# Slots of a macaron block: where the layer norm runs, and how tokens and attention weights are turned

## The chip, the cores and the metric

The kernel runs on one core of a Trainium2 chip. The metric is the device time of one execution in microseconds (us). The kernel before took 2431.72 us, the median of three runs (2429.35 to 2433.34). One further execution was profiled; its time is 2431.14 us and the profile's span of it is 2429.4 us.

## The reference

The input x is 16 sequences of 512 tokens of width 256, all in float32. The block is a macaron: x gets half of a slot FFN, then causal attention, then half of the same slot FFN again; each of the three works on a layer norm of x without scale and shift.

```python
x = x + 0.5 * ffn(layernorm(x)); x = x + attn(layernorm(x)); x = x + 0.5 * ffn(layernorm(x))

def ffn(h):                                      # h: 512 tokens x 256, 16 slots, 16 heads of 16
    o = slot_query + mha(slot_query, h, h)       # slots attend to tokens ("dispatch")
    o = o + experts(layernorm(o))                # one gated expert of width 1024 per slot
    return mha(h, o, o)                          # tokens attend to the slots ("combine")
```

What the change touches is the dispatch: for every sequence, 256 rows of scores (16 heads times 16 slots) against 512 tokens, a softmax over the tokens, and the weighted sum of the normalized tokens.

## The kernel before, in words

`ffn(n, ...)` runs twice, as n = 0 ahead of the attention and as n = 1 behind it. Each has three stages: the slots (`slots_and_experts`, its first `with` block), the experts (`experts`), and the combine (`combine`). The change is in the slots stage; a few of its lines reach the others.

**Slots stage.** A loop over i takes one sequence b at each step, in a software pipeline three steps deep. A sequence x[b] lies in SBUF with tokens on the 128 partitions (4 groups of 128 tokens, 256 wide). For one sequence the stage does this:

- `token_stats` (L194, L195): VectorE's mean and variance of each group of 128 tokens, four pairs of instructions. For n = 1 the attention has done them already. `pair_rstd` turns the variances of two sequences into 1/std: a square root by ScalarE (L199) and a reciprocal by VectorE (L200).
- `normalized` (L218): h = (x - mean) * rstd, four VectorE instructions of 128x256.
- `width_first` (L226 to L230): the normalized sequence is turned so that its width lies on the partitions: eight transposes of 128x128 by TensorE into two PSUM banks `p_hT`, copied to `hT` by ScalarE (first half, L228) and by VectorE (second half, L230).
- `slot_weights`: for each half c of the 256 score rows, TensorE's scores `p_ds` (L436), VectorE's row maximum (L438), two small GpSimd instructions (L439, L440), ScalarE's exponential with row sums (L441); then VectorE's reciprocal (L443) and GpSimd's scaling of both halves (L445). The result `at` has score rows on the partitions.
- `weights_transposed` (L454 to L460): `at` is turned so that tokens lie on the partitions: eight transposes of 128x128 by TensorE, four to a PSUM bank, copied to `atT` by ScalarE (L458) and VectorE (L460).
- `slot_sums` (L467): TensorE's weighted sums `p_z`, from `h` and `atT`; VectorE copies them to `zT` (L469).

Every fourth sequence `gathered` (L481) multiplies four sequences' sums by the value weights into `moT`. `hT` is kept for the combine: `queries(b)` (L359) makes the tokens' queries from it.

**Order.** TensorE's order is the order of the program text. The other engines and the DMA queue of SyncE (SP) are ordered by a planner in the slots stage. Nearly all DMAs are issued on SP, which takes them one after another. A DMA holds one of eight completion semaphores in turn, so an issue also waits until the DMA eight places ahead of it has landed.

**Weights of the experts.** Each expert has three matrices of 1 MB; eleven buffers hold them. `EARLY` of the buffers exist from the stage's start and are filled there by `load.more(EARLY)`; the other `BUFS - EARLY` lie in memory that the slots stage uses, and are filled when it has ended. The expert loop takes `queries` as fillers, one to an expert (`2 <= e < 11`, and from `e >= NS` on).

**The attention**, between the two, already turns its weights in another way: VectorE transposes 32x32 blocks (L866), and `move` (L889) places them by 16 DMAs from SBUF to SBUF, each from 32 partitions to 32 partitions, 160 KB. Its `enter` (L746) normalizes with ScalarE, with `scale = rstd` and `bias = -mean * rstd`.

Of the kernel before, what the change touches and what calls it, by code (L numbers as in the profile page):

```python
# [9 lines left out]
F32 = mybir.dt.float32  # L10
AF = mybir.ActivationFunctionType
ALU = mybir.AluOpType
# [18 lines left out]
EW = NC * F  # L31
EARLY, BUFS = 7, 11

# [14 lines left out]
def macaron_kernel(ctx: ExitStack, tc: tile.TileContext, a: dict, out: bass.AP):  # L48
# [19 lines left out]
    def by_width(t):  # L68
        return t.rearrange("p (c s) -> p c s", c=NC)

    xin = a["attn_x"].rearrange("b (t p) d -> b p t d", p=P)
# [26 lines left out]
    with tc.tile_pool(name="setup", bufs=1) as su:  # L98
# [44 lines left out]
        for c in range(NC):  # L143
# [6 lines left out]
                            pattern=[[-1, S]], channel_multiplier=1)  # L150
    def more_constants(su):

# [12 lines left out]
        for k, nm in enumerate(("e_b1", "e_bg")):  # L165
            br = su.tile([NS * NQ, QW], F32, tag=f"br{k}", name=f"br{k}", bufs=1)
            nc.sync.dma_start(br, a[nm].rearrange("e (q i) -> (e q) i", q=NQ))
            brs.append(br)
# [17 lines left out]

    mvs, rstds = {}, {}

# [13 lines left out]
    def pair_stats(g):  # L202
        for b in range(g * PB, (g + 1) * PB):
            for t in range(NT):
                token_stats(b, t)

    def pair_rstd(g, parts=1):
        rstds[g] = small.tile([P, PB * NT], F32, tag=f"rstd{g}", name=f"rstd{g}", bufs=1)
        n = PB * NT // parts
        for i in range(parts):  # L210
            inverse_std(rstds[g][:, i * n:(i + 1) * n], mvs[g][:, i * n:(i + 1) * n, 1], n, f"g{g}_{i}")

    def normalized(pool, b, bufs):

        h = pool.tile([P, NT, D], F32, tag="h", name=f"h{b}", bufs=bufs)
        for t in range(NT):
            i = (b % PB) * NT + t
            nc.vector.tensor_scalar(h[:, t, :], xs[b][:, t, :], mvs[b // PB][:, i, 0:1],  # L218
                                    rstds[b // PB][:, i:i + 1], ALU.subtract, ALU.mult)
        return h  # L220

    def width_first(h, b, hT, c):

        pt = ps(f"p_hT{b}_{c}")
        for t in range(NT):
            nc.tensor.transpose(pt[:, t * P:(t + 1) * P], h[:, t, c * P:(c + 1) * P], ident)  # L226
        if c == 0:
            nc.scalar.copy(hT[:, c, :], pt)  # L228
        else:
            nc.vector.tensor_copy(hT[:, c, :], pt)  # L230

# [71 lines left out]
    def slots_and_experts(n, ss, load, w, wvm, rows, hTs, kT, vT):  # L303
# [49 lines left out]
        def queries(b):  # L353

            pqs = []
            for c in range(NC):
                pq = ps(f"p_cq{b}_{c}")
                for k in range(NC):
                    nc.tensor.matmul(pq, w["c_Wq"][:, k, c * P:(c + 1) * P], hTs[b][:, k, :],  # L359
                                     start=(k == 0), stop=(k == NC - 1))  # L360
                pqs.append(pq)
            qT = by_width(place(b, f"cq{n}_"))
            for c in range(NC):
                bias = bcol[:, R_CBQ + c:R_CBQ + c + 1]
                if c == 0:
                    nc.scalar.activation(qT[:, c, :], pqs[c], AF.Identity, bias=bias)
                else:
                    nc.vector.tensor_scalar(qT[:, c, :], pqs[c], bias, 1.0, ALU.add, ALU.mult)
            hTs[b] = qT

        with tc.tile_pool(name=f"disp{n}", bufs=2) as dp:
            hs, ats, zT = {}, {}, None
            constants = more_constants(dp) if n == 0 else None
            tail = None
            load.more(EARLY)

            def norm(b):

                if b >= NB:
                    return  # L380
                if b % PB == 0 and (n == 0 or b >= 2 * PB):
                    pair_rstd(b // PB, PB if b == 0 else 1)
                hs[b] = normalized(dp, b, 4)
                if n == 0 and b % PB == 0 and b + PB < NB:
                    pair_stats(b // PB + 1)

            if n == 0:
                pair_stats(0)
            norm(0)
            norm(1)  # L390
            for i in range(NB + 2):
                if i < NB:
                    hTs[i] = by_width(place(i, f"hT{n}_"))
                    for c in range(NC):
                        width_first(hs[i], i, hTs[i], c)
                if i > 2:
                    atT = weights_transposed(dp, i - 2, ats.pop(i - 2))
                if 0 <= i - 1 < NB:
                    ats[i - 1] = slot_weights(dp, i - 1, hTs[i - 1])
                if i == 2:  # L400
                    atT = weights_transposed(dp, 0, ats.pop(0))
                if i == 5 and n == 0:
                    constants()
                if i > 0:
                    norm(i + 1)
                if i >= 2:
                    b = i - 2
                    if b % GB == 0:
                        if b > 0:
                            gathered(b // GB - 1, zT, moT, wvm)  # L410
                        zT = dp.tile([P, NC, FH, GB, NS], F32, tag="zT", name=f"zT{b}", bufs=1)
                    slot_sums(b, zT, hs.pop(b), atT)
                    if b == NB // 2:
                        tail = half_of_slots(0)
                    if b == NB // 2 + 1:
                        tail()
            queries(0)
            gathered(NB // GB - 1, zT, moT, wvm)
            queries(1)
            tail = half_of_slots(1)  # L420
        with tc.tile_pool(name=f"late{n}", bufs=1) as lw, tc.tile_pool(name=f"exp{n}", bufs=2) as ep:
            load.late = lw
            load.more(BUFS - EARLY)
            queries(2)
            queries(3)
            tail()
            experts(ep, load, w, hET, oT, kT, vT, [lambda b=b: queries(b) for b in range(4, NB)])

    def slot_weights(dp, b, hT):
        at = dp.tile([P, NC, S], F32, tag="at", name=f"at{b}")  # L430
        rsum = small.tile([P, NC], F32, tag="rsum", name=f"rsum{b}")
        mx = small.tile([P, NC], F32, tag="nmx", name=f"nmx{b}")
        for c in range(NC):
            psc = ps(f"p_ds{b}_{c}")
            for k in range(NC):
                nc.tensor.matmul(psc, qk[:, k, c * P:(c + 1) * P], hT[:, k, :], start=(k == 0), stop=(k == NC - 1))  # L436

            nc.vector.tensor_reduce(mx[:, c:c + 1], psc, AX.X, ALU.max)  # L438
            nc.gpsimd.tensor_tensor(mx[:, c:c + 1], mx[:, c:c + 1], sbias[:, c:c + 1], ALU.add)  # L439
            nc.gpsimd.tensor_tensor(mx[:, c:c + 1], sbias[:, c:c + 1], mx[:, c:c + 1], ALU.subtract)  # L440
            nc.scalar.activation(at[:, c, :], psc, AF.Exp, bias=mx[:, c:c + 1], accum_out=rsum[:, c:c + 1])  # L441
        rinv = small.tile([P, NC], F32, tag="rinv", name=f"rinv{b}")
        nc.vector.reciprocal(rinv, rsum)  # L443
        for c in range(NC):
            nc.gpsimd.tensor_scalar(at[:, c, :], at[:, c, :], rinv[:, c:c + 1], 1.0, ALU.mult, ALU.mult)  # L445
        return at

    def weights_transposed(dp, b, at):
        atT = dp.tile([P, NT, FH * NS], F32, tag="atT", name=f"atT{b}", bufs=1)
        for t0 in range(0, NT, 2):  # L450
            pt = ps(f"p_atT{b}_{t0}")
            for t in range(2):
                for c in range(NC):
                    nc.tensor.transpose(pt[:, t * 256 + c * P:t * 256 + (c + 1) * P],  # L454
                                        at[:, c, (t0 + t) * P:(t0 + t + 1) * P], ident)
            dst = atT[:, t0:t0 + 2, :].rearrange("p t q -> p (t q)")
            if t0 == 0:
                nc.scalar.copy(dst, pt)  # L458
            else:
                nc.vector.tensor_copy(dst, pt)  # L460
        return atT

    def slot_sums(b, zT, h, atT):
        pz = ps(f"p_z{b}")
        for c in range(NC):
            for t in range(NT):
                nc.tensor.matmul(pz[:, c * 256:(c + 1) * 256], h[:, t, c * P:(c + 1) * P], atT[:, t, :],  # L467
                                 start=(t == 0), stop=(t == NT - 1))
        nc.vector.tensor_copy(zT[:, :, :, b % GB, :], pz.rearrange("p (c h q) -> p c h q", c=NC, h=FH))  # L469

# [18 lines left out]
    def experts(ep, load, w, hET, oT, kT, vT, fillers):  # L489
# [77 lines left out]
        for e in range(NS + 3):  # L567
# [7 lines left out]
            if 0 <= e - 3 < NS:  # L575
                onto_slots(e - 3)
            if (2 <= e < 11 or e >= NS) and fillers:
                fillers.pop(0)()
# [139 lines left out]
    def attention(qp, wq, wk, wv, wo, cos, sin, row):  # L718
# [4 lines left out]
        nu = len(units)  # L723
        hTs, hs, qs, ks, vs, oTs, prTs, shifts, stds = {}, {}, {}, {}, {}, {}, {}, {}, {}

# [7 lines left out]
        def scales(g, std):  # L733

            n = PB * NT
            rstds[g] = small.tile([P, n], F32, tag=f"rstd{g}", name=f"rstd{g}", bufs=1)
            shifts[g] = small.tile([P, n], F32, tag="shift", name=f"shift{g}", bufs=2)
            nc.vector.reciprocal(rstds[g], std)
            nc.vector.scalar_tensor_tensor(shifts[g], mvs[g][:, :, 0], -1.0, rstds[g], ALU.mult, ALU.mult)

# [317 lines left out]
```

## Time and profile before

| what | value |
|---|---|
| median of three runs | 2431.72 us |
| time of the profiled execution | 2431.14 us |
| its span | 2429.4 us |
| slots stage, n = 0: last `p_z` ends | 174.5 us |
| slots stage, n = 1: first `p_hT` starts, last `p_z` ends | 2014.0 us, 2166.2 us |
| DMA moved | 323.18 MB, mean 133 GB/s |
| mean granted TensorE clock | 0.983 |

The page of the profile has the busy time of each engine, the span in 40 slices, the DMA queues, the chain of work that ended last, and the costliest groups of instructions. A group line reads: source line, engine, operation, out<-in, partitions x elements, number, then busy time and mean of one instruction, then the idle time ahead of it and what ended it. A float32 matmul of the program stands as two instructions in the trace: "x8" for `p_ds` is four matmuls (a transpose stands as one).

### The profile page before, as it was taken

To read this page: it belongs to the slowest core of one execution; us is meant where nothing else is said; L and a number is where in the kernel's file an instruction comes from. 1 tells how busy PE (TensorE), PEld (TensorE's weight loads), DVE (VectorE), ACT (ScalarE), POOL (GpSimd) and SP (SyncE) were. 2 spreads that over 40 slices of the span, in tenths; PEclk is the share of its full clock that TensorE was granted. 3 is DMA by queue.
4 is the path that set the end of the run, shared out by engine and by line. 5 is a ranking of instruction groups with operands and counts; after the bars stand their busy time and mean duration, and the time that the engine had idled before them with its cause. 6 is when DMAs were issued, how large, how long until landed. Compare 5 with 4: busy or idle time off the path is not lost.

```text
span 2429.4 us, 42489 instructions
## 1 busy us (share of the span) xinstructions
PE 2349.0 (97%) x14720; PEld 1475.6 (61%) x14720; DVE 1777.7 (73%) x4687; ACT 1069.4 (44%) x2919; POOL 1065.3 (44%) x1692
## 2 busy tenths in 40 slices
PE   7999889899999999999999999999999979999899
PEld 5765479555555655555656555555555546765488
DVE  8542278778888888888888888888888855542287
ACT  4332233345555555554545545545555433322233
POOL 2220044555564655555656555655556432210053
PEclk9999999999999999999999999999999989999899
DMA  8009852246464555455554545454646454019734
GB/s 308 1 9 370 332 142 78 44 88 138 93 134 102 125 114 117 110 121 112 115 123 104 129 107 120 107 125 102 134 94 138 102 125 167 1 72 397 276 109 135
DMA packets 142477, 323.18 MB, mean 133 GB/s; under 512 B 37236, under 2 KB 84408, under 8 KB 134072
## 3 DMA queue, kind: packets, MB, share of 16 engines
q1 hardware_dynamic: 141676, 319.93, 49.5%
q8 instruction: 117, 1.92, 0.3%
q14 instruction: 96, 0.79, 0.1%
q10 hardware_dynamic: 588, 0.54, 0.1%
HBM read 135.84 MB, written 16.78 MB: 63 GB/s over the span
## 4 chain that ended last, share of the span: by engine, by line
PE 83%; DVE 3%; DMA 2%; SPq 2%; ACT 1%; issue 1%; POOL 0%; DVEq 0%; POOLq 0%; ACTq 0%
PE p_as L831 12%; PE p_av L900 11%; PE p_k L771 9%; PE p_v L792 9%; PE p_q L771 8%; PE p_ay L916 8%; PE p_cq L359 5%; PE p_cy L648 4%; PE p_u L509 2%; PE p_cs L617 2%; PE p_z L467 2%; PE p_ds L436 2%; SPq L889 2%; PE p_y L536 1%; DVE sq L866 1%; PE p_catT L638 1%
## 5 line engine op out<-in xcount | busy, mean ns | idle before, releaser
L851 POOL TENSOR_SCALAR pr<-pr,ars 128x512 f32<-128x512 f32 (+3 forms) x1024 | 523.5, 532 | 655.0 <-DVE ars L848 655.0
L843 ACT ACTIVATE pr<-pr,amn 128x512 f32<-128x512 f32 (+3 forms) x1024 | 561.6, 550 | 462.6 <-DVE amn L839 462.5
L839 DVE CUSTOM_DVE_ANT_0 pr<-p_as,causal 128x512 f32<-128x512 f32 (+3 forms) x1024 | 434.3, 485 | 97.8 <-PE p_as L831 96.5
L866 DVE STREAM_TRANSPOSE sq<-pr 128x768 f32<-128x768 f32 (+2 forms) x448 | 381.6, 906 | 17.4 <-issue 12.8
L831 PE MATMUL p_as<-k,q 32*128 32x512 f32 (+3 forms) x4096 | 332.5, 449 | 3.6 <-POOL k L782 3.6
L900 PE MATMUL p_av<-prT,v 128*64 128x512 f32 (+3 forms) x2048 | 296.7, 443 | 20.4 <-DMA prT<-sq 14.7
L831 PEld LDWEIGHTS p_as<-k,q 32*128 32x128 f32 x4096 | 180.2, 185 | 131.6 <-issue 52.0
L900 PEld LDWEIGHTS p_av<-prT,v 128*64 128x64 f32 x2048 | 141.7, 139 | 181.5 <-issue 158.6
L792 PEld LDWEIGHTS p_v<-wv,ahT 128*128 128x128 f32 x1024 | 189.2, 190 | 98.7 <-issue 45.8
L792 PE MATMUL p_v<-wv,ahT 128*128 128x256 f32 x1024 | 248.5, 386 | 0.0
L916 PE MATMUL p_ay<-wo,aoT 128*128 128x256 f32 x1024 | 238.3, 386 | 0.1
L771 PE MATMUL p_k<-ahT,wk 128*128 128x512 f32 x512 | 236.9, 605 | 0.0
L771 PE MATMUL p_q<-ahT,wq 128*128 128x512 f32 x512 | 230.5, 592 | 0.2 <-ACT ahT L757 0.2
L916 PEld LDWEIGHTS p_ay<-wo,aoT 128*128 128x128 f32 x1024 | 189.3, 190 | 31.3 <-ACT aoT L907 0.6
L843 ACT ACTIVATION_READ_ACCUMULATOR pr<-pr,amn 128x1 f32 x1024 | 191.5, 187 | 0.0
L907 ACT ACTIVATE aoT<-p_av,bcol 128x512 f32<-128x512 f32 x128 | 88.0, 687 | 197.9 <-PE p_av L900 197.8
L771 PEld LDWEIGHTS p_k<-ahT,wk 128*128 128x128 f32 x512 | 92.1, 189 | 126.2 <-issue 114.2
L595 POOL TENSOR_TENSOR kbd<-kT,own 128x256 f32<-128x256 f32 x32 | 19.7, 618 | 309.7 <-DVE kT L562 273.5
L771 PEld LDWEIGHTS p_q<-ahT,wq 128*128 128x128 f32 x512 | 97.1, 190 | 95.8 <-issue 86.3
L648 PE MATMUL p_cy<-vw,catT 128*128 128x256 f32 x512 | 122.5, 383 | 3.0 <-ACT catT L640 3.0
L467 PE MATMUL p_z<-atT,h 128*128 128x256 f32 x512 | 120.2, 389 | 3.6 <-ACT atT L458 3.6
L795 ACT COPY v<-p_v 128x512 f32<-128x512 f32 x128 | 73.4, 573 | 104.9 <-PE p_v L792 104.9
(153 smaller groups left out, 3305.2 us busy)
## 6 DMA issues: line engine op xcount, KB each, us to landing
prT<-sq SPq DMA_DIRECT2D x1024, 160.0 KB
w<-in_e_W_dram SPq DMA_DIRECT2D x64, 1024.0 KB
w<-in_e_Wg_dram SPq DMA_DIRECT2D x32, 1024.0 KB
out_dram<-x SPq DMA_DIRECT2D x64, 256.0 KB
xl<-in_attn_x_dram SPq DMA_DIRECT2D x16, 512.0 KB
xl<-out_dram SPq DMA_DIRECT2D x16, 512.0 KB
x<-in_attn_x_dram SPq DMA_DIRECT2D x15, 512.0 KB
wq<-in_attn_Wq_dram SPq DMA_DIRECT2D x16, 64.0 KB
```

Of the source, the lines that this page charges most:

```text
L359: nc.tensor.matmul(pq, w["c_Wq"][:, k, c * P:(c + 1) * P], hTs[b][:, k, :], start=(k == 0), stop=(k == NC - 1))
L467: nc.tensor.matmul(pz[:, c * 256:(c + 1) * 256], h[:, t, c * P:(c + 1) * P], atT[:, t, :], start=(t == 0), stop=(t == NT - 1))
L648: nc.tensor.matmul(py[:, t * D:(t + 1) * D], atT[:, c, t * P:(t + 1) * P], vws[b][:, c, :], start=(c == 0), stop=(c == NC - 1))
L771: nc.tensor.matmul(pq, self.w[:, k, at:at + P], hTs[self.b][:, k, :], start=(k == 0), stop=(k == NC - 1))
L792: nc.tensor.matmul(pv[:, t * 256:(t + 1) * 256], hTs[b][:, k, (t0 + t) * P:(t0 + t + 1) * P], wv[:, k, hg * HG * DQ:(hg + 1) * HG * DQ], s ...
L831: nc.tensor.matmul(banks[j][:, at:at + w], q[n][j * 32:(j + 1) * 32, i * P:(i + 1) * P], k[n][j * 32:(j + 1) * 32, :w], start=(n == 0), st ...
L839: nc.vector.tensor_tensor_reduce(out=self.at(i, j), in0=banks[j][:, at:at + w], in1=causal[:, S - w:], scale=-1.0 / math.sqrt(DQ), scalar= ...
L843: nc.scalar.activation(self.at(i, j), self.at(i, j), AF.Exp, bias=self.mn[:, i, j:j + 1], scale=-1.0, accum_out=self.rs[:, i, j:j + 1])
L851: nc.gpsimd.tensor_scalar(self.at(i, j), self.at(i, j), self.rs[:, i, j:j + 1], 1.0, ALU.mult, ALU.mult)
L866: nc.vector.transpose(view(self.sq, j * blocks * SQ + dst[0] * SQ, [(blocks * SQ, nh)] + [(s * SQ, n) for s, (_, n) in zip(dst[1:], of)] + ...
L900: nc.tensor.matmul(po[j * DQ:(j + 1) * DQ, :].rearrange("d (a f) -> d a f", a=NSQ)[:, :, t * SQ:], vs[u][:, t, head * DQ:(head + 1) * DQ], ...
L916: nc.tensor.matmul(py[:, t * D:(t + 1) * D], oTs[u][:, pair, (t0 + t) * P:(t0 + t + 1) * P], wo[:, hg * (HG // 2) + pair, :], start=(pair ...
```

## The change

It does five things in the slots stage.

1. The layer norm of all sequences but the first two goes from VectorE to ScalarE (`normalized`), as in the attention; `pair_shift` makes the bias.
2. `at` is no longer turned by TensorE. A new class `Squares` has VectorE transpose 32x32 blocks of a 128x1024 tile into `sq`, writes `sq` to a buffer in device memory by one DMA of 512 KB (`away`, three buffers), and reads it back by four DMAs of 128 KB, each to 32 partitions. Each partition gets four pieces of 1 KB from one read.
3. `h` is turned in the same way into `hT`, for sequences from the fifth on for n = 0 and from the third on for n = 1; the first ones (`direct`) still go through TensorE. `hT`, and what reads it, is laid out by blocks of 32.
4. VectorE, ScalarE, GpSimd and SP follow the program text in the loop (`manual_schedule`). The statistics of sequence i + 4 stand in step i. `zT` is copied by ScalarE.
5. `EARLY` goes from 7 to 6, and the early expert matrices are issued one to a step, in steps 1 to 6, where all seven were issued ahead of the loop. `queries(0)` stands ahead of the last `p_z`, one `queries` more is made before the expert loop, and one filler less is in it.

Step i of the new loop issues on SP, in this order: the four reads of `hT` of i + 1, the write of `at` of i - 1, the write of `h` of i + 2, the four reads of `at` of i - 1, and in steps 1 to 6 one expert matrix. The core of the diff:

```diff
-EARLY, BUFS = 7, 11
+EARLY, BUFS = 6, 11
...
+    class Squares:
+        def __init__(self, pool, away, name, src, outer, inner):
+            n = outer * inner * SQ
+            sq = pool.tile([P, NSQ, n], F32, tag="sq", name=f"sq{name}", bufs=2)
+            nc.vector.transpose(sq.rearrange("p k (i o x) -> p o i k x", i=inner, o=outer),
+                                src.rearrange("p (o i k y) -> p o i k y", o=outer, i=inner, k=NSQ))
+            self.mem = away.tile([P, NSQ, n], F32, tag="away", name=f"away{name}")
+            nc.sync.dma_start(self.mem, sq)
+
+        def onto(self, dst):
+            for k in range(NSQ):
+                nc.sync.dma_start(dst[k * SQ:(k + 1) * SQ].rearrange("y (a f) -> y a f", a=NSQ),
+                                  self.mem.rearrange("(a y) k f -> k y a f", a=NSQ)[k])
...
+            if b < PB:
+                nc.vector.tensor_scalar(h[:, t, :], xs[b][:, t, :], mvs[b // PB][:, i, 0:1], rstd,
+                                        ALU.subtract, ALU.mult)
+            else:
+                nc.scalar.activation(h[:, t, :], xs[b][:, t, :], AF.Identity, bias=shifts[b // PB][:, i:i + 1],
+                                     scale=rstd)
...
-            load.more(EARLY)
...
+            with tc.manual_schedule(engines={mybir.EngineType.DVE, mybir.EngineType.Activation,
+                                             mybir.EngineType.Pool, mybir.EngineType.SP}):
+                for i in range(NB + 2):
+                    if i + 1 in turned:
+                        t = place(i + 1, f"hT{n}_")
+                        hTs[i + 1] = by_squares(t)
+                        turned.pop(i + 1).onto(t)
+                    if i + 1 < direct:
+                        width(i + 1)
+                    if i + 2 < NB:
+                        hs[i + 2] = normalized(dp, i + 2, 5)
+                    if 0 <= i - 1 < NB:
+                        back = Squares(dp, away, f"a{i - 1}", at.rearrange("p c s -> p (c s)"), NC, NT)
+                    stats = [(i + 2 * PB, t) for t in range(NT)] if n == 0 and i + 2 * PB < NB else []
+                    for one in stats[:1]:
+                        token_stats(*one)
+                    def between():
+                        if direct <= i + 2 < NB:
+                            turned[i + 2] = Squares(dp, away, f"h{i + 2}", hs[i + 2].rearrange("p t d -> p (t d)"),
+                                                    NT, NC)
+                    if i < NB:
+                        at, scaled = slot_weights(dp, i, hTs[i], between)
+                    if 0 <= i - 1 < NB:
+                        atT = dp.tile([P, NT * FH * NS], F32, tag="atT", name=f"atT{i - 1}", bufs=2)
+                        back.onto(atT)
...
+                    for one in stats[1:3]:
+                        token_stats(*one)
+                    if i < NB:
+                        scaled()
+                    for one in stats[3:]:
+                        token_stats(*one)
...
+                    if 0 < i <= EARLY:
+                        load.more()
...
+                        if b == NB - 1:
+                            queries(0)
+                        slot_sums(b, zT, hs.pop(b), ats.pop(b))
...
-            if (2 <= e < 11 or e >= NS) and fillers:
+            if (2 <= e < 10 or e >= NS) and fillers:
```

`between` runs after the first half's exponential in `slot_weights`, so VectorE's order in a step is: transpose of `at` of i - 1, one pair of statistics, maximum of the first half, transpose of `h` of i + 2, maximum of the second half, two pairs of statistics, reciprocal, one pair.

## The prediction

> **What bounds the kernel now.** I read the page's engine line first, then the chain of work that ended last in order of time, then the timeline of SP's issues, then the busy time and DMA share by stretches.
>
> ```profile
> PE 2349.0 (97%) x14720; PEld 1475.6 (61%) x14720; DVE 1777.7 (73%) x4687; ACT 1069.4 (44%) x2919; POOL 1065.3 (44%) x1692
> ```
>
> TensorE (PE) is busy nearly all the time, so work taken off it pays at once if nothing else becomes late. The chain in the second slots stage (n = 1):
>
> ```profile
> 2035.24 0.87 PE p_hT L226 x8
> 2036.12 0.87 PE p_atT L454 x8
> 2036.99 3.44 PE p_ds L436 x8
> 2040.42 3.45 PE p_z L467 x16
> 2043.88 0.87 PE p_hT L226 x8
> ...
> 2162.47 3.72 PE p_z L467 x16
> ```
>
> A sequence costs 2043.88 - 2035.24 = 8.64 us, all of it PE, and 1.74 of it are the two turns. The stage ends with the last p_z, at 2166.2; in the first (n = 0) it is 170.78 + 3.72 = 174.5. Behind it:
>
> ```profile
> 170.78 3.72 PE p_z L467 x16
> ...
> 274.23 10.53 DMA w<-in_e_Wg_dram
> ```
>
> So the experts end on their weights, not on PE. The first late weight is issued when the stage's memory is free, 4.6 us after the last p_z, and the DMAs then run full to 284.8: 41 MB in 105.7 us, 2.6 us each. What counts is therefore **when the last p_z ends**, and every MB that is not loaded before. SP's timeline:
>
> ```profile
> 39.01 0.59 SPq L167 DMA_DIRECT2D br<-in_e_bg_dram  x1
> ...
> 179.12 0.33 SPq L291 DMA_DIRECT2D w<-in_e_Wg_dram  x1
> ```
>
> and, from the attention, where 16 DMAs of 160 KB go to 32 partitions each:
>
> ```profile
> 713.03 10.04 SPq L889 DMA_DIRECT2D prT<-sq  x16
> ```
>
> At the start SP is taken up with the input and some twenty small constants until 39.6 us. The columns of the next view end with granted clock, DMA share and GB/s:
>
> ```profile
> 719.00:721.00 2.00, 2.00 (x15) 0.88 (x8) 1.93 (x7) 0.56 (x2) 2.00 (x4) 1.00 1.02 213
> 240.00:260.00 20.00, 20.00 (x180) 9.79 (x178) 5.34 (x15) 5.74 (x11) 0.00 (x0) 1.00 0.99 377
> ```
>
> With the DMAs full, 32-partition moves give 213 GB/s, weights to 128 partitions 377.
>
> **PE.** Removed: 16 turns of at per stage and 12 (n = 0) or 14 (n = 1) of h: 58 x 0.87 = 50.5 us. A step is then 3.44 + 3.45 = 6.9 us. p_av, which already reads blocks of 32, takes 4.46 us for 10240 columns (x32 in the chain), no slower a column than p_ds (3.44 for 4096), so I cost the new layout at nothing.
>
> **VectorE.** A 128x1024 transpose is 1.20 us in the attention (L866). In a step: two of these (2.4), two maxima (0.69 each), and for n = 0 four pairs of statistics (0.41 + 0.17 each); the norm and three copies leave it. More telling is a loop in the given order: transpose of at, maximum, transpose of h, maximum (1.2 + 0.69 + 1.2 + 0.69 = 3.8), then from the second maximum over GpSimd, the exponential, the reciprocal and the scaling back to the next transpose of at. In the tail of before this took 2161.14 - 2158.06 = 3.1 us. Sum 6.9 to 7.0; with the pair of statistics inside the loop 7.6 for n = 0. So VectorE alone allows 7.0 and 7.6, and the saving of PE would mostly stand.
>
> **ScalarE.** Four norms at about 0.52 (three in 1.57 us in the attention, L746), two exponentials with sums (0.88 each), one copy (0.69): 4.6 us; for n = 0 two table loads of 1.28 and a root per two steps make 6.0. Below 7.6, so it is covered; were it not, at most 0.4 a step.
>
> **SP, the step that decides.** Per step SP issues, strictly in order, four reads of hT, the write of at, the write of h, then four reads of at, which wait until the write of at has landed. The next write of at stands behind the next four reads of hT. The loop from one write of at to the next is **landing of the write + eight issues**; the issue of the second write is hidden in the landing, and the transposes are ready earlier (with 7.4 us steps VectorE has at ready some 5 us ahead).
>
> - An issue: 10.04 / 16 = 0.63 us for the 32-partition DMAs; the 512 KB loads xl of the combine take 0.37 + 0.04 of gap = 0.41. The new reads have 32 partitions like the one and come from memory like the other; I take the middle, 0.52. Eight: 4.2 (3.3 to 5.0).
> - Landing, from the completion marks in the trace: a 256 KB write out_dram<-x issued alone at 584.42 had landed after 2.14 us, its bytes in 0.75 us of full DMA. Twice the bytes: 2.9 alone. Right behind four 128 KB reads (the four first ones of x landed 2.1 to 2.8 after issue) it comes to some 3.2. Bounds 2.8 and 4.2.
>
> Without a weight a step is 3.2 + 4.2 = 7.4 us: over PE's 6.9, under the old 8.64. For n = 0 VectorE's 7.6 stands above it.
>
> **A weight in the step.** In steps 1 to 6 a 1 MB weight is issued behind the reads of at, so the reads of hT and the next write queue behind it. That DMAs of this queue wait for each other the trace shows: a 256 KB write issued 0.43 us after a 512 KB load landed after 4.6 us (at 2404.68), not 2.1. The first weight of before landed 5.2 us after its issue. Issued 2.6 us ahead of the write it lands 2.6 after the write's issue; the four reads and the write itself add about 3.0: landing 5.6. Such a step is 5.6 + 4.2 + 0.5 = **10.3 us**, longer than the old 8.64. Before, the seven weights were issued at once and cost PE nothing.
>
> **Sum, first stage.** SP reaches the first write of at not before 39.6. Second write: 39.6 + 2.8 + 2.1 + 0.5 = 45.0. It has a weight right ahead (5.9 to land), and the first reads of hT follow: 45.0 + 5.9 + 2.1 + 0.5 + 2.1 = 55.6. Five loaded steps: 107.1. Eight of 7.6: 167.9. To the end: landing 3.2, four issues 2.1, the last read's landing 1.8, p_z 3.7: 178.7, against 174.5: **+4.2**.
> **Second stage.** The first scores end at 2024.2, and scaling (3.85) and transpose put the first write at 2029.8. Next: + 3.2 + 2.1 + 0.5 + 2.1 = 2037.7. Six loaded steps: 2099.5. Eight of 7.4: 2158.7. End: 2169.5 against 2166.2: **+3.3**.
> **Experts.** One early MB less: 2 x 2.6 = **+5.2**. The moved queries gain nothing, as the experts end on DMAs; were these not the end, a query is 3.44 us.
> Together +12.7 on the profiled 2431.14: **2444 us** (the median is 0.6 above the profiled time).
>
> With issue 0.41 and landing 2.8 the steps are 7.6, 7.0 and 9.5 (loaded), the stages end 2.1 and 6.9 earlier, the sum is -3.8: 2427. With 0.63 and 4.2 (reads at 213 GB/s hold up the write) they are 9.2 and about 12, the stages end 29 and 31 later: 2496.
>
> The row of 213 GB/s above has 32 partitions on both sides; a read from memory to 32 is not in the trace. The Trainium skill, page "SBUF — State Buffer", section "Door 1: The DMA port swizzle", says that partitions 0 to 31 reach only half of the ports, about 218 GB/s. By that, the eight reads of a step (1.05 MB) need 4.8 us, more than their issues, a step would be about 8.0 and my estimate of the sum some 17 us more; by the row of 377 GB/s they need 2.8 and hide.
>
> **Rivals.**
> 1. *The transfers hide* (faster). If a waiting read holds up less than I think, or the weights are spread over idle DMA time, the steps are VectorE's 7.6 and 7.0 throughout. The first stage then saves some 13 us, the second 22, less 5: about 2401. For it: DMA share is 0.01 in this stage before (80 to 160 us), and 2.1 MB per step at 377 GB/s is 5.6 us of 7.0. Against it: SP's order and the two landings in series.
> 2. *It cancels*: shorter plain steps pay for longer loaded steps, within 0.2% (about what a measurement of this kernel can tell from no change): 2431.
> 3. *The reads run at the 32-partition rate*: steps of 8.0 to 9.2, 2460 to 2496.
>
> Decided by one number, the plain step: at 7.0 and with loaded steps of 9.5 the change breaks even; below, it gains.
>
> **Chances.** Forecast (2437 to 2460) 0.48; cancels 0.15; hides 0.25; rate 0.12. Slower by over 0.2%: 0.60; within: 0.15; faster: 0.25. The range, 2405 to 2482, leaves out the far part of rival 1 (0.12) and of rival 3 (0.05).
>
> **What would show it.** Steps of p_ds in the chain: 10 us in steps 2 to 7 and 7.4 to 7.6 later, PE waiting on DMAs of hT and atT (right), or 6.9 to 7.0 with VectorE or PE in the chain (rival 1). SP should wait on the landing of "away" writes for about 3 us a step. The first read of at near 42 us; weights landing 5 us after issue. I am wrong if the reads are issued in 0.4 us, if a 512 KB write lands in 2.5 us behind reads, or if a weight does not hold up what follows.

## The result and the profile after

| | before | after |
|---|---|---|
| median beside each other, us | 2432.53 (2429.35 to 2434.44) | 2469.10 (2466.77 to 2474.31) |
| ratio, 95% interval | | 1.0161 [1.014, 1.0182] |
| time of the profiled execution, its span | 2431.14, 2429.4 | 2474.31, 2472.6 |
| mean granted TensorE clock | 0.983 | 0.974 |
| last `p_z` ends, n = 0 | 174.5 | 195.1 |
| first `p_hT` starts, last `p_z` ends, n = 1 | 2014.0, 2166.2 | 2034.2, 2209.0 |
| DMA moved | 323.18 MB | 384.00 MB |

The kernel became 1.6% slower. All of it lies in the two slots stages: the first ends 20.6 us later, the second is 174.8 us long instead of 152.2 (22.6 more), what lies between them (1839.1 against 1839.5) and behind the last `p_z` (263.6 against 263.2) is unchanged. 20.6 + 22.6 = 43.2, the difference of the two spans. The profiled execution is the slowest of its four; the medians differ by 36.6.

The engine line of the page after, to be held against the one of before:

```profile
PE 2320.4 (94%) x14256; PEld 1431.5 (58%) x14256; DVE 1758.6 (71%) x4557; ACT 1112.7 (45%) x3007; POOL 1064.3 (43%) x1692
```

TensorE's busy time did fall, by 28.6 us, and the kernel is slower all the same: what was taken off TensorE is less than the waits that came. It fell by less than the 50.5 us of turns that went, among other things because matmuls that stayed took longer: the same 256 instructions of `p_ds` were busy for 126.1 us in place of 118.2, the 512 of `p_z` for 124.3 in place of 120.2. The chain of work that ended last, in the second stage, in one step with a weight (start, length, what):

```profile
2058.66 0.02 SPq L259
2058.67 0.03 issue
2058.70 7.74 DMA awaya<-sqa
2066.45 0.02 issue
2066.46 0.32 SPq L263
...
2068.25 0.43 SPq L325
...
2070.56 6.88 DMA hT<-awayh
2077.43 0.14 issue
2077.57 5.38 PE p_ds L505 x8
```

Where before each sequence was 8.64 us of TensorE, the chain is now made of transfers: 7.74 us for the write of turned attention weights, then reads of `atT` (L263), then the weight (L325), then 6.88 us for the last read of `hT`, and only then the scores. The waits of SP in the steps 2 to 7 of that stage (engine, line, what it waited for: us in total, times, longest):

```profile
SPq L263 <- DMA awaya<-sqa: 40.3, 6, 7.6
```

6.7 us a step go into waiting for a write to land. And the busy time by stretches; the first row is these six steps, the second five plain ones behind them (the columns end with granted clock, DMA share and GB/s):

```profile
2058.70:2134.60 75.90, 49.68 (x208) 29.11 (x208) 23.83 (x36) 24.88 (x55) 12.88 (x37) 0.93 0.80 249
2142.40:2184.00 41.60, 37.94 (x193) 24.49 (x192) 22.52 (x40) 21.32 (x45) 10.58 (x30) 1.00 0.84 256
```

The reader is to see two things. A loaded step takes 75.9 / 6 = 12.65 us, a plain one 8.3. And in both the 16 DMA engines are busy for 80 to 84% of the time, though they move only 249 to 256 GB/s; with weights alone it was 377 GB/s at a share of 0.99 (in the kernel before) and 413 at 1.03 (in run e2 below). For the same busy time about a fifth less is moved.

The trace also has every packet (the piece that one DMA engine moves at a time) with its size and length. Summed over the 16 engines and divided by 16, a loaded step holds 4.1 us of reads (1 KB packets, mean 63 ns), 2.7 us of writes (4 KB, 167 ns) and 3.2 us of the weight: 10.0 of the 12.65. A plain one has 4.2 and 2.7: 6.9 of 8.3.

### The profile page after: what moved, and what is told of

Same layout as the page of the kernel before. It is cut to its first block, busy times and chain, and to the rows that moved or that the text cites. A ratio compares the mean times of both kernels' runs of the same rounds, so it can differ in the third digit from the quotient of the medians.

```text
span 2472.6 us, 41964 instructions
## 1 busy us (share of the span) xinstructions
PE 2320.4 (94%) x14256; PEld 1431.5 (58%) x14256; DVE 1758.6 (71%) x4557; ACT 1112.7 (45%) x3007; POOL 1064.3 (43%) x1692
## 2 busy tenths in 40 slices
DMA packets 184238, 384.00 MB, mean 155 GB/s; under 512 B 41876, under 2 KB 118744, under 8 KB 175832
## 4 chain that ended last, share of the span: by engine, by line
PE 80%; DMA 9%; DVE 4%; SPq 4%; ACT 1%; issue 1%; POOL 0%; DVEq 0%; ACTq 0%; POOLq 0%
PE p_as L892 12%; PE p_av L961 11%; PE p_v L853 9%; PE p_k L832 9%; PE p_ay L977 9%; PE p_q L832 9%; DMA awaya<-sqa 5%; PE p_cq L393 4%; PE p_cy L710 4%; PE p_u L571 2%; PE p_cs L679 2%; SPq L263 2%; PE p_z L529 1%; PE p_y L598 1%; PE p_catT L700 1%
## 5 line engine op out<-in xcount | busy, mean ns | idle before, releaser
L927 DVE STREAM_TRANSPOSE sq<-pr 128x768 f32<-128x768 f32 (+2 forms) x448 | 381.6, 906 | 16.7 <-issue 12.7
L529 PE MATMUL p_z<-atT,h 128*128 128x256 f32 x512 | 124.3, 398 | 45.7 <-DMA atT<-awaya 36.1
L505 PE MATMUL p_ds<-hT,qk 128*128 128x512 f32 x256 | 126.1, 640 | 24.7 <-DMA hT<-awayh 24.7
L529 PEld LDWEIGHTS p_z<-atT,h 128*128 128x128 f32 x512 | 99.3, 199 | 78.3 <-issue 46.8
```

The lines of the kernel that those rows point to most:

```text
L505: nc.tensor.matmul(psc.rearrange("p (a n) -> p a n", a=NSQ), qk[:, k, c * P:(c + 1) * P], hT[:, k], start=(k == 0), stop=(k == NC - 1))
L529: nc.tensor.matmul(pz[:, c * 256:(c + 1) * 256].rearrange("p (c g i) -> p c g i", c=NC, g=NSQ), h[:, t, c * P:(c + 1) * P], atT[:, t], sta ...
L927: nc.vector.transpose(view(self.sq, j * blocks * SQ + dst[0] * SQ, [(blocks * SQ, nh)] + [(s * SQ, n) for s, (_, n) in zip(dst[1:], of)] + ...
```

## Theories and experiments

**A.** A step is the landing of the write plus eight issues, in SP's order: the theory of the prediction. **B.** The step is set by the time that all its packets take on the shared DMA engines, in whatever order they are issued. **C.** The order that is now given to VectorE, ScalarE and GpSimd makes the loop late. The kernels below were compared with the kernel before on the same chip; the ratios are to it.

**Run e1, the write ahead of the reads.**

```diff
-                    if i + 1 in turned:          # the four reads of hT
-                        ...
                     if i + 2 < NB:
                         hs[i + 2] = normalized(dp, i + 2, 5)
                     if 0 <= i - 1 < NB:
                         back = Squares(dp, away, f"a{i - 1}", ...)
+                    if i + 1 in turned:
+                        ...
```

> Edit: in each step the write of at is issued ahead of the four reads of hT instead of behind them; nothing else moves. Theory A (the loop on SP decides: landing of the write of at, then eight issues, where 4.3 us and 8 x 0.46 us were measured in plain steps, 7.7 us landing in steps with a weight): four issues leave the loop, a plain step falls from 8.0 to 7.0 to 7.6 (the next limit is VectorE's loop), a step with a weight from 12.3 to about 10.3; the time falls by about 30 us, to 2439. Theory B (the DMA engines are simply full, DMA share 0.8 to 0.9 in these steps, and the order of the issues does not matter): steps stay within 0.5 us of 8.0 and 12.3, the time falls by 8 us at most. Theory C (the given order of the compute engines, with VectorE and ScalarE waiting on TensorE in their order, is what lengthens the steps): no change within 5 us.

Measured: 2460.45 us, ratio 1.0124 [1.0099, 1.0149], some 9 us less than the change, though the two intervals touch. Most plain steps became 6.6 to 8.4 (three were 10.1 to 12.8), but the loaded ones stayed at 9.7 to 13.8, and the landing of the write in them grew to between 7.0 and 11.4 us. The order matters little, as B says.

**Run e2, the weights behind the loop.**

```diff
-                    if 0 < i <= EARLY:
-                        load.more()
+                    if i == NB:
+                        load.more(EARLY)
```

> Edit: the six early expert matrices are issued together in step 16, behind the last reads of at, and not one to a step in steps 1 to 6. Theory A: all steps are plain ones of 8.0 us, six times 4.3 us less per stage (26), the matrices then land partly behind the stage's end and cost some 5 us of it back per stage: about -40 us, 2429. Theory B: the bytes of the weights leave the full steps, 6 x 2.6 us less per stage, and return at the end: -15 to -20 us. Theory C: no change of the steps, and later weights: 5 to 15 us slower.

Measured: **2422.95 us, ratio 0.997 [0.996, 0.998]**: 46 us less than the change, and 0.3% faster than the kernel before. The same six steps of the second stage, by stretches, and SP's waits in them:

```profile
2046.80:2094.50 47.70, 43.51 (x208) 27.81 (x208) 23.82 (x36) 24.38 (x55) 12.70 (x36) 1.00 0.84 264
```

```profile
SPq L263 <- DMA awaya<-sqa: 18.2, 6, 3.6
```

A step is 7.95 us in place of 12.65, and TensorE is busy for 91% of it in place of 65%. In this stage the six weights cost 4.7 us each where they stood: more than the 2.6 of an undisturbed MB, and more than their packets' 3.2. The second stage is now 143.9 us long (152.2 before), the first ends at 178.6 (174.5 before). So turning through memory does gain, in the second stage, 8.3 us; what made the kernel slower is where the weights went.

**Run e3, `h` by TensorE.** `direct = NB`: only `at` goes through memory.

> Edit: h of all sequences is turned by TensorE as before the change; only the attention weights go through VectorE and memory. Theory A: the loop on SP has only four issues and an emptier queue (landing 2.8 + 4 x 0.46 + write, 4.7 us, with a weight about 8.7), so plain steps are TensorE's 7.75 us: about 2420, below the kernel before. Theory B: half the bytes, the same steps as in A. Theory C: VectorE and ScalarE still wait in their given order: steps of 8 us and more, and a time of 2440 or more.

Measured: 2440.92 us, ratio 1.0053 [1.0033, 1.0074]. Half of the loop's bytes and issues are gone and plain steps are 7.8 (TensorE's own 6.9 + 0.87), yet a loaded step is mostly still 8.3 to 11.4 (one is 14.3) with landings of 6 to 9 us, and the forecast of A is missed by 21 us. The time is the one that C gave (2440 or more), but not by C's way, since the plain steps are below 8. DMA share fell to 0.61 (2060 to 2120 us): here the engines are not full, and the step with a weight is long all the same. B alone does not explain that; a write that lands late behind the weight would.

**Run e4, the planner orders the engines.** The `manual_schedule` of the slots loop is taken away.

> Edit: only TensorE's order is given; the planner orders VectorE, ScalarE, GpSimd and SP in the slots stage as before the change. The planner puts SP's four reads of at ahead of the four reads of hT and both writes and the weight ahead of both; the loop on SP keeps its eight issues and the landing. Theory A: the same steps, 2469 within 10 us (a weight now lies ahead of the reads of at, too). Theory B: the same, 2469 within 5 us. Theory C: the steps fall to TensorE's 6.9 to 7.5 us, 2440 or less.

Measured: 2446.49 us (2433.48 to 2453.76), ratio 1.0068 [1.0049, 1.0088], about 23 us less than the change, between the expectations. The planner puts the writes and the weight ahead of the reads; landings of writes fall to 3.8 to 5.5 (one is 6.9), the reads of `at` behind the weight take 5 to 8 us, and loaded steps are 9.4 to 12.2. So the given order is worth a part of the loss, and no order that was tried makes a weight in the step free.

**Run e5, both edits** (e1 and e2).

> The two edits before together: no weight inside the loop (all six are issued behind the last step), and the write of the turned attention weights is issued ahead of the four reads of hT. Theory A (a step is the write's landing plus eight issues, all in SP's order): the write no longer stands behind four issues of 0.47 us nor behind their 0.5 MB, so a plain step falls from about 7.9 to TensorE's 6.9 or VectorE's 7.6, some 0.5 to 0.9 us a step over 26 steps: about 2403 to 2412 us, ratio 0.990 to 0.993 to the kernel before. Theory B (the DMA engines' throughput sets the step: 2.1 MB a step at 260 to 300 GB/s is 7 to 8 us in whatever order): no gain over the version with the weights at the end alone, 2419 to 2426.

Measured: 2423.04 us, ratio 0.9979 [0.9968, 0.999], no better than e2 alone: the number that B gave. But the waits show another reason than B's. SP's waits over the whole second stage, first of this run, then of the changed kernel:

```profile
SPq L259 <- DVE sqa L256: 32.4, 16, 6.4
...
SPq L263 <- DMA awaya<-sqa: 6.2, 5, 2.6
```

```profile
SPq L263 <- DMA awaya<-sqa: 65.2, 16, 7.6
```

SP hardly waits for landings any more (in e2 it was 41.4 us in this stage); it waits for VectorE's transpose. The loop has a new bound, and from the fourth step of the second stage on one step alone stands out, 12.8 us against 6.6 to 8.4; in the first stage four are 10.2 to 13.0. The one of 12.8 in the chain:

```profile
2104.49 0.88 PE p_o L350 x4
2105.36 0.02 issue
2105.39 0.43 DVE o L353
...
2107.96 0.04 DVE hE L363
...
2108.30 1.25 DVE sqa L256
```

The first half of the slots' layer norm (L353 to L363) needs a result of TensorE and a root of ScalarE, and VectorE's next transpose waits behind it: that makes the step 12.8 us long. That is theory C, visible once the weights are gone; what it is worth, run e10 shows.

**Run e6, reads to 128 partitions.**

```diff
-                nc.sync.dma_start(dst[k * SQ:(k + 1) * SQ].rearrange("y (a f) -> y a f", a=NSQ),
-                                  self.mem.rearrange("(a y) k f -> k y a f", a=NSQ)[k])
+                nc.sync.dma_start(dst.rearrange("y (a f) -> y a f", a=NSQ)[:, k], self.mem[:, k])
```

> The changed kernel with its four reads per turned tile kept at 128 KB and 1 KB packets each, but every read goes to all 128 partitions (one 1 KB block of each) where it went to 32 with four blocks each. The blocks are thus not moved between partitions: that part of the computation is left out. Count of issues, bytes and packet sizes are unchanged. If the slow reads to 32 partitions (14.6 to 18.7 bytes per ns and engine, against 21.8 for loads to 128) lengthen the landings (rival 3 of the prediction), the loaded steps fall from 12.5 to about 11 and the plain ones from 7.9 to about 7.2: some 30 us less, about 2440. If bytes and order alone count (theory A and B), the time stays within 8 us of 2469.

Measured: 2457.12 us, ratio 1.0123 [1.0094, 1.0152], some 9 us less than the change by the ratios, though the intervals touch. The kernel leaves out the moving of the blocks between partitions. Six loaded steps and five plain ones of the second stage:

```profile
2047.50:2117.90 70.40, 50.67 (x205) 29.31 (x203) 24.33 (x37) 25.23 (x56) 12.75 (x37) 0.90 0.78 264
2125.50:2165.30 39.80, 38.11 (x220) 24.91 (x224) 21.93 (x41) 21.31 (x44) 10.59 (x30) 1.00 0.74 265
```

A 1 KB packet took 50 to 52 ns in place of 63, the reads of a step 3.3 us in place of 4.1, and a loaded step 11.7 in place of 12.65. The 32 partitions of a read have a price, 0.8 us of DMA time a step, but a small one: rival 3 of the prediction explains about a quarter of the loss.

**Run e7, the blocks are moved by the writes.** Four writes of 128 KB from 32 partitions, one read of 512 KB to 128, the weights behind the loop.

```diff
-            nc.sync.dma_start(self.mem, sq)
+            for k in range(NSQ):
+                nc.sync.dma_start(self.mem.rearrange("(k y) a f -> y k a f", k=NSQ)[:, :, k], sq[k * SQ:(k + 1) * SQ])
...
-            for k in range(NSQ):
-                nc.sync.dma_start(dst[k * SQ:(k + 1) * SQ].rearrange("y (a f) -> y a f", a=NSQ),
-                                  self.mem.rearrange("(a y) k f -> k y a f", a=NSQ)[k])
+            nc.sync.dma_start(dst.rearrange("y (a f) -> y a f", a=NSQ), self.mem)
```

> Weights behind the loop, and the moving of blocks is done by the writes: four writes of 128 KB from 32 partitions each, to their turned place in memory, then one read of 512 KB to 128 partitions with 4 KB packets; the result is the same. Per step still ten issues, but between the landing of a write and the next write of at stand only two reads and four writes (six issues in place of eight), and the waiting read is one. Theory A: about 2 x 0.47 = 0.9 us less per step where the loop decides, 2405 to 2415. Theory B: the packets of the reads are larger (4 KB, 24 bytes per ns and engine) but those of the writes smaller (1 KB), so nothing changes: 2419 to 2427. If a write of 1 KB packets lands later than one of 4 KB by 1 us or more, it is slower: above 2430.

Measured: 2426.14 us, ratio 0.9985 [0.9972, 0.9998], the same as e2 within the intervals. Two issues fewer between landings gain nothing: in the second stage the writes of `at` now land mostly after 4.2 to 5.7 us where e2 had 3.3 to 4.5. The packets of a plain step sum to 6.7 us (writes of 1 KB 3.1, reads of 4 KB 3.6), against 6.5 in e2 (writes 2.65, reads 3.9): what the reads gain the writes lose. A is wrong here in its form: fewer issues do not shorten the step, the landing grows.

**Run e8, the weights on another queue.** The six early weights are issued by ScalarE at the same places (`nc.scalar.dma_start` in `more`).

> The changed kernel with its six early weights issued at the same places but by ScalarE, to its own DMA queue, in place of SP's. Theory A (a transfer stands behind the weight in SP's queue): the writes no longer queue behind the 1 MB, the landing in loaded steps falls from 7.7 towards 4, the loaded steps from 12.5 to about 8.5, and 11 of them save some 40 us: about 2430. Theory B (the 16 DMA engines are shared and full, whichever queue feeds them): a weight still costs 2.6 to 4 us of DMA time in its step, loaded steps 11 to 12.5: 2455 to 2470.

Measured: 2463.05 us, ratio 1.015 [1.0122, 1.0178], as B says. The chain of that kernel in a loaded step:

```profile
2066.83 8.46 DMA w<-in_e_W_dram
2075.29 0.02 SPq L263
...
2076.65 7.14 DMA atT<-awaya
2083.80 0.14 issue
2083.93 1.19 PE p_z L530 x2
```

Some writes now land in 3.5 to 4.0 us although a weight is under way, but a read of 128 KB takes 7.14 us instead of 3. Loaded steps are 9.8 to 15.1 us. So a transfer can be late behind a weight of another queue. But this run does not part A from B, because it brings a wait that the changed kernel does not have. In the trace the two queues take the same eight completion semaphores in turn, and SP has to wait for a weight's landing before it can issue a read (waits of SP, 2034 to 2120 us):

```profile
SPq L263 <- DMA w<-in_e_W_dram: 8.0, 1, 8.0
...
SPq L263 <- DMA w<-in_e_Wg_dram: 5.9, 1, 5.9
```

In the first stage there are four such waits, together 20.3 us; in the changed kernel there is none in either stage. What the queue alone is worth stays open.

**Run e9, one read of 4 KB packets.** The weights stay in the loop; `self.mem` is read by one DMA of 512 KB, as in e7, but written as in the changed kernel, so the moving of the blocks between partitions is left out.

```diff
-            for k in range(NSQ):
-                nc.sync.dma_start(dst[k * SQ:(k + 1) * SQ].rearrange("y (a f) -> y a f", a=NSQ),
-                                  self.mem.rearrange("(a y) k f -> k y a f", a=NSQ)[k])
+            nc.sync.dma_start(dst.rearrange("y (a f) -> y a f", a=NSQ), self.mem)
```

> The changed kernel, weights in the loop, with one read of 512 KB per turned tile (4 KB packets to 128 partitions) in place of four of 128 KB (1 KB packets to 32 partitions); the blocks are not moved between partitions, that part of the computation is left out. Theory A (landing plus issues in SP's order): between the landing of a write and the next one stand two issues in place of eight, 2.8 us less a step: loaded steps 12.5 to about 9.7, plain ones to the 7.2 of TensorE, about 2428 us. Theory B (the sum of the packets' time on the 16 engines: per loaded step reads 4.1, writes 2.7, weight 3.2, and some 2.5 idle): only the reads shrink, 4.1 to 2.6, loaded steps about 11.1, about 2445. If neither the packet size nor the issues count, it stays at the 2457 of the reads to 128 partitions.

Measured: 2435.21 us (2423.96 to 2443.74), ratio 1.0024 [1.0008, 1.004], between A and B. Loaded steps are about 10.4 us, plain ones go down to 6.6. The busy time of five loaded steps of the second stage:

```profile
2046.30:2100.40 54.10, 41.03 (x185) 24.18 (x185) 19.49 (x31) 20.57 (x45) 10.62 (x30) 0.94 0.84 292
```

The engines move 292 GB/s in place of 249. Six issues fewer (2.8 us) and larger packets together gave 2.2 us a step; the landing of the write rose from about 7.7 to 9.1 in these five steps; the write now comes sooner behind the weight, which may be why. Against e6, whose reads also go to 128 partitions, larger packets and fewer issues give 24 us by the ratios; this run does not part the two.

**Run e10, small work moved out.** e5, and the constants' turning and the first half of the slots' layer norm go to the end of the loop.

```diff
-                    if i == 5 and n == 0:
+                    if i == NB and n == 0:
                         constants()
...
-                        if b == NB // 2:
+                        if b == NB - 2:
                             tail = half_of_slots(0)
-                        if b == NB // 2 + 1:
+                        if b == NB - 1:
                             tail()
```

> The version with the weights behind the loop and the write ahead of the reads of hT, and in addition the turning of the small constants (from step 5) and the first half of the slots' layer norm (from step 10) moved to the end of the loop, so that VectorE's given order no longer has them ahead of a transpose. Theory C (VectorE's order puts each such insertion on the loop: steps of 13.0 at 79.9 and 12.8 at 2096.9 against 7.4 around them): 5 us less in each stage for the latter and 5 in the first for the former, 15 less in all: about 2408. If what is moved returns behind the loop, 2418 to 2424.

Measured: **2410.17 us, ratio 0.9927 [0.9909, 0.9945]**, 13 us less than e5, about what C gave, but not where C put it. The first stage ends at 165.9 (178.1 in e5, 174.5 before), 12 us sooner. The second is 143.9 us long against 144.5 in e5: its step of 12.8 us is now 8.3, but 2.3 of these 4.5 us come back in the steps behind it and 1.6 ahead of it. And what follows the last `p_z` takes 259.5 us against 262.5. So freeing VectorE's order paid in the first stage and hardly in the second. Three sequences of the second stage in the chain:

```profile
2050.31 3.67 PE p_ds L505 x8
2053.98 3.45 PE p_z L529 x16
2057.43 3.43 PE p_ds L505 x8
2060.86 1.03 PE p_mo L543 x64
2061.90 3.67 PE p_z L529 x16
2065.56 0.13 issue
2065.69 3.67 PE p_ds L505 x8
2069.36 3.47 PE p_z L529 x16
```

This is what the change could have been: 3.43 + 3.45 us a sequence with TensorE in the chain and the DMAs hidden behind it. Over the stage a sequence still takes 7.8 us (`p_ds` from 2026.18 to 2127.95, 13 sequences).

**Run e11, constants by GpSimd.** e10, with the small loads of `more_constants` issued by GpSimd.

> As the run before, and the small constants of the start are issued by GpSimd to its own queue in place of SP. SP is free of them some 10 us earlier than 39.6, and the first write of at goes out when VectorE has turned it, at about 30. If the 21.6 us of the second step of the first stage (TensorE waits 12.5 for the first atT) come from SP's list of small loads, they fall to about 12, and the time is some 10 us below that of the run before, about 2398 to 2410; if the queue of the input is the limit instead, no gain.

Measured: 2406.67 us, ratio 0.991 [0.9891, 0.9928]; the interval overlaps that of e10. The first write of `at` goes out at 33.0 in place of 39.5 but takes 5.9 us to land, and TensorE's wait for the first `atT` falls from 12.8 to 8.3 us. But the first stage ends no sooner, at 166.4 against 165.9, so a gain from the moved loads is not shown. It is the fastest kernel of these runs, 22 us below the one before.

**Run e12, the kernel before with six early weights.** `EARLY, BUFS = 6, 11`.

> The kernel before with six early weights per stage where it had seven, nothing else. The prediction put one MB less at the start at 2 x 2.6 = 5.2 us more (2436), as the experts end on the DMAs. The traces of before and after show the same distance from the last p_z to the last late weight (110.3 and 110.6 us), which speaks for no difference: 2429 to 2432.

Measured: 2428.85 us, ratio 1.0002 [0.9989, 1.0014]: no difference. The 20 us behind the last `p_z` of the first stage, in the kernel before, in this run, and in e2, which still has all its six to load when the loop ends:

```profile
174.50:194.50 20.00, 19.29 (x161) 10.15 (x163) 7.47 (x18) 4.91 (x7) 0.56 (x2) 1.00 0.57 212
```

```profile
174.80:194.80 20.00, 19.29 (x161) 10.19 (x163) 7.47 (x18) 4.91 (x7) 0.00 (x0) 1.00 0.68 266
```

```profile
178.60:198.60 20.00, 19.29 (x161) 10.13 (x164) 6.78 (x17) 5.50 (x8) 0.56 (x2) 1.00 1.03 413
```

The DMA engines had 43% of 20 us to spare there, room for three MB, and TensorE was busy for 19.29 us in each case. e2 also uses the 15 us ahead of the last `p_z` (share 0.67). That fits its weights being loaded so late at no cost.

## Why the prediction was right or wrong

Right: the sign, the mechanism that a loaded step is longer than the old 8.64 us and a plain one shorter, and the place (SP waits for the landing of the write, TensorE for `hT` and `atT`). Too small by a factor of three: the amount, 12.7 us forecast, 36.6 between the medians and 43.2 between the spans. By the prediction's own steps:

| step | forecast | measured |
|---|---|---|
| an issue | 0.52 | 0.47 (0.42 + 0.05), in loaded steps now and then 0.8 to 1.1 |
| first two writes, n = 0 | 39.6, 45.0 | 40.1, 45.3 |
| landing, plain step | 3.2 | 2.6 to 4.6, mostly 3.6 to 4.4 |
| plain step, n = 0, n = 1 | 7.6, 7.4 | 8.0, 7.9 |
| landing with a weight | 5.6 | 6.8 to 8.5, mean 7.7 |
| loaded step | 10.3 | 11.3 to 13.8 |
| first stage to its end | +4.2 | +20.6 |
| second stage | +3.3 | +22.6 |
| one early MB less | +5.2 | 0 (e12) |

**The step that failed is the landing behind a weight.** The prediction put it at 5.6 us: the weight's 2.6 from the rate of weights alone, and 3.0 for reads and write. Measured are 7.7. In the loaded steps this is 61.9 in place of 51.5 us for n = 0 (with 2.1 more for the first) and 75.9 in place of 61.8 for n = 1, together 26.6 of the 35.7 us by which the two stages missed their forecast. The error was to price each transfer as if it had the engines for itself: the bytes under way were the reads of `at`, the weight, the reads of `hT` and both writes, and together they went at 249 GB/s, not 377. Put as sums of packets, 4.1 + 2.7 + 3.2 = 10.0 us, where the prediction counted 2.1 MB at 377 GB/s as 5.6 and the weight as 2.6. The 2.6 was itself a miscount: the weight that lands at 284.8 in the kernel before is the 37th behind the last `p_z`, not the 41st, so one took 2.85 us; the 41st lands at 295.0.

**The plain step** was short by 0.4 to 0.5 us, together 6.8 us over both stages. The landing was mostly 0.4 to 1.2 longer, by B for the same reason; and once a stage VectorE's order held up the transpose (9.9 us at 137.1 in the first), which the prediction had not seen: it counted VectorE's work in a step, but not what stands in its order and waits for other engines.

**The experts** end on their weights, but not on the number of them. The prediction took the share of DMA from one stretch (240 to 260 us) for the whole time from 179 to 285; the row above shows 0.57 in the first 20 us. What counts there is when the last `p_z` ends: the weight that the chain waits for lands 110.5 us after it (110.3 before, 109.8 in e2, where nearly all weights land behind it).

**What was costed at nothing:** the layout by blocks was free (`p_ds` 3.43, `p_z` 3.45 in e10). ScalarE's and VectorE's time was mostly covered as long as the transfers set the step; in e5 VectorE's order was late next, with most steps of the second stage at 7.0 to 7.6 where the sum had 7.0. The norm by ScalarE was not tried by itself.

**The rivals.** "The transfers hide" came near to what e10 reached (2410; 2401 was given). One of its two conditions, the weights in idle DMA time, is what e2 and e10 do; that VectorE's order must also be free of other work it did not name. "The reads at the 32-partition rate" had the right range (2460 to 2496), but in good part by luck, as it has about a quarter of the cause (e6). The Trainium skill, page "SBUF — State Buffer", section "Door 1: The DMA port swizzle", gives partitions 0 to 31 half of the ports and about 218 GB/s, by which the eight reads of a step need an estimated 4.8 us, if they go one behind the other. By its table, partitions 64 to 127 lie at the other half of the ports. Of the four reads of a tile two go to these, and they are issued about 0.47 us apart and land 2.9 us or more after their issue, so they overlap, and the 4.8 us that the prediction took from this page does not follow for them. Measured, as packet times, are 4.1 us to 32 partitions and 3.3 to 128, a factor of 1.25, with 1 KB packets in both; no run here has reads to one half alone.

**What stays open:** packet size and number of issues were changed together in e9; a weight was never tried ahead of the loop, as the kernel before has it; whether a weight on another queue would cost less without the shared semaphores (e8); which of the two moves of e10 gained; and why a weight costs 4.7 us in a step when its packets need 3.2 is only argued: the engines idle for 2.6 us of a loaded step and for 1.4 of a plain one, perhaps because SP's next issues wait for a landing that the weight has made late.

## What to carry to other kernels

Price a step of a loop that goes through memory by the packets of everything that shares the DMA engines in it, at the lengths that packets of that size have in a busy stretch, and only then by the order of issue; an issue that is saved can come back as a longer landing. A bulk load that is put into such a loop can cost more than its own time, as here, so first look for a stretch where the DMA share is low and the consumer is not waiting: here it lay right behind the loop. And in an order that is given by hand, look at what each instruction in it waits for: one that needs another engine's result holds up what stands behind it, and that costs time where the loop has no slack (in e10 in one stage of two).

## What the runs showed of the hardware

- A TensorE that has waited can run slower when it comes back. In the loaded steps of the second stage the stretch around `p_ds` at 2077.57, behind a wait of 2.35 us, has a granted clock of 0.69, its neighbours 1.00, and the same eight instructions took 5.37 us in place of 3.43 without a wait:

```profile
2064.00:2077.50 13.50, 7.36 (x24) 4.39 (x24) 3.84 (x6) 5.99 (x14) 2.12 (x6) 1.00 0.87 284
2077.50:2083.00 5.50, 5.37 (x8) 2.03 (x8) 3.11 (x4) 1.03 (x3) 0.38 (x2) 0.69 0.49 145
```

  After a wait of 2.17 us, at 2065.78, `p_ds` took 3.67. So a wait on a DMA can cost more than its length.
- Busy DMA engines have no fixed rate: 249 GB/s at a share of 0.80 with tiles of 1 and 4 KB packets and a weight, 292 at 0.84 with 4 KB packets, 413 at 1.03 with weights alone.
- A DMA of another engine's queue does not always run beside SP's for nothing: with the weight on ScalarE's queue a 128 KB read landed after 7.1 us in place of 3 (e8).
